# Ends of the expert blocks as a lane of jobs of their own, token-place sums on GpSimd, first projection one tick later: a two-layer transformer on one Trainium2 core

## The chip, the cores and the metric

The kernel runs on one core of a Trainium2 chip. The metric is device time in microseconds (us) of one execution; less is better. PE is TensorE, DVE is VectorE, ACT is ScalarE, POOL is GpSimd, SP is SyncE, which issues most DMAs. Each engine works through its own queue in order and waits for others by semaphores.

## The reference

Input is x, 2 sequences of 1024 tokens with 128 features, float32. Four sublayers follow one another, each with a residual and a layer norm behind it:

```python
x = _layernorm(x + _L0_attn_ref(x, ...))   # retention, 8 heads, decay, group norm, gate
x = _layernorm(x + _L0_ffn_ref(x, ...))    # causal attention of 16 heads of 8, then experts
x = _layernorm(x + _L1_attn_ref(x, ...))   # full attention of 16 heads of 8
x = _layernorm(x + _L1_ffn_ref(x, ...))    # product with a ternary 128x128 matrix
```

The second holds the part that is changed. After its attention it does, with a one-hot choice of one expert of four for every token:

```python
x = x + mla_attention(rmsnorm(x, norm1_w), Wq, Wdkv, Wuk, Wuv, Wo, ln_g, ln_b)
x = x + moe(rmsnorm(x, norm2_w), gate_w, gate_b, W1, b1, W2, b2)
...
h = jax.nn.relu(jnp.einsum('btd,ehd->bteh', x, W1) + b1)
y = jnp.einsum('bteh,edh->bted', h, W2) + b2
return jnp.einsum('bted,bte->btd', y, onehot)
```

## The kernel before, in words

Tokens go in tiles of 128, four tiles to a block of 512; block (b, k) is half k of sequence b. The retention runs first, chunk by chunk. From about 240 us on the kernel is a chain of **ticks** (chain_tick, line 553). A tick has one piece of scores for row maxima on PE (score, line 391; the maxima on DVE, lines 417 for pieces with the diagonal and 422 for whole ones), one piece of shifted, transposed scores that lies 7 pieces behind (shifted, line 455) with its exponentials on ACT (line 477), a mask on POOL for diagonal pieces of the causal attention (line 485), and the product of the piece before it with the values (line 502), whose result ACT copies out (tile part, two buffers, line 513) and POOL adds to oT (line 514). At the end of a group of heads come four transposes o_ps (line 524), a reciprocal and o_tok on DVE (lines 527, 528). Once a step's maxima are whole, ACT copies them to m_rows and SP brings them into qT by a DMA (line 444). All products go through eight PSUM banks in a ring: PE can't write a bank before DVE or ACT has read what was in it eight slots ago.

There are 208 pieces: ticks 0 to 79 start the causal attention's pieces, 80 to 207 the full attention's, where a block's full attention starts at 80 (b = 0) or 144 (b = 1). Ahead of every tick side_work (line 1393) steps the jobs of two lanes, heavy first, then light. A job is a generator; what it yields is the number of ticks until its next step. Only the first job of a lane steps, once in a tick unless it yields 0, and not before the jobs in its after list are done; a due time forces steps. Whatever a step issues stands in the engines' queues ahead of that tick's own work. Heavy holds experts(b, k) (line 1137) for the four blocks, light holds mla_inputs (the projections of sequence 1), attn_inputs (line 1290, which transposes the normalised block for the full attention at line 1302, projects it and spreads queries and keys by DMAs on SP, line 273) and outputs.

The stages of experts: project (transposes of o_tok, line 1059, then the product), residual xa on DVE; rmsnorm_T (line 238: square on POOL; sum ss on DVE, rstd and xn on POOL; transposes); gate product, choice of the expert oh and residual acc; places (line 1064), which counts with two products where each token goes in a list sorted by expert, in small DVE operations (lines 1078 to 1134); four scatters from POOL (line 1191), weights loaded by SP (line 1183); the sorted rows back, seven tiles of two products each (lines 1216 to 1238), the rows out. Then the **end** (lines 1260 to 1272): four gathers from POOL, an add to acc and the moments on DVE, rstd on POOL, and a tick later the normalising on DVE (line 228), which writes the input of the full attention.

By the program's order, the ticks of the ends are:

| block | gathers | add and moments | normalising | transposes of attn_inputs |
|---|---|---|---|---|
| (0,0) | 48, 49 | 50 | 51 | 52 |
| (0,1) | 73, 74 | 75 | 76 | 77 |
| (1,0) | 103, 104 | 105 | 106 | 107 |
| (1,1) | 133, 134 | 135 | 136 | 137 |

Blocks follow one another in the heavy lane: (0,0) steps from tick 22 to 52, (0,1) from 52 to 77, (1,0) from 77 to 107, (1,1) from 107 to 137. The counts of places come in ticks 29, 58, 84 and 114, the sums from them in the three ticks after.

Of the kernel before, what the change touches and what calls it, by code (L numbers as in the profile page):

```python
# [14 lines left out]
P = 128  # L15
# [49 lines left out]
def block_kernel(  # L65
# [66 lines left out]
    def col(name, i=0, rows_=P):  # L132
        at, _ = COLS[name]
        return cols_sb[:rows_, at + i : at + i + 1]
# [5 lines left out]
        nc.gpsimd.tensor_tensor(r, r, nhalf[:, :n], ALU.pow)  # L140
        return r

    def moments(parts):

        n = len(parts)
        st = small.tile([P, n, 6], F32, tag=f"st{n}", name="st")
        mv = small.tile([P, n, 2], F32, tag=f"mv{n}", name="mv")
        for i, part in enumerate(parts):
            nc.vector.bn_stats(st[:, i, :], part)
            nc.vector.bn_aggr(mv[:, i, :], st[:, i, :])  # L150
        return mv
# [48 lines left out]
    def flat(t):  # L200
        return t.rearrange("p c d -> p (c d)")
# [19 lines left out]
    def stats(parts):  # L221

        mv = moments(parts)
        return mv, rstd(mv[:, :, 1], len(parts), 1e-5)
# [7 lines left out]
    def tiles(t):  # L232
        return [t[:, c, :] for c in range(t.shape[1])]

    def scratch(tag, name, shape=(P, NC, P)):
        return scratch_of[0].tile(list(shape), F32, tag=tag, name=name)
# [819 lines left out]
    def project(src, w, name, got, tag):  # L1056
# [4 lines left out]
        yield 1  # L1061
        got["py"] = by_tile(oT, w, f"{name}_ps")

    def places(oh, found):

        def tiny(shape, name, dtype=F32):  # L1070
            return small.tile([P, *shape], dtype, tag=name, name=name, bufs=2)

        ps = slot("places")
        flat_oh = oh.rearrange("p c e -> p (c e)")
        mm(ps[:, : NC * NE], ahead, flat_oh)
        mm(ps[:, NC * NE : 2 * NC * NE], ones, flat_oh)
        got = tiny([2, NC, NE], "counts")
        nc.vector.tensor_copy(
            got.rearrange("p a c e -> p (a c e)"), ps[:, : 2 * NC * NE]
        )  # L1080
        rank_, total = got[:, 0], got[:, 1]
        for c in range(1, NC):
            nc.vector.tensor_tensor(total[:, c], total[:, c], total[:, c - 1], ALU.add)
        yield 1
        nc.vector.tensor_tensor(rank_[:, 1:], rank_[:, 1:], total[:, : NC - 1], ALU.add)
        some = tiny([NE, NC], "some")
        nc.vector.tensor_tensor(
            some, total[:, NC - 1].unsqueeze(2).to_broadcast([P, NE, NC]),
            filled.unsqueeze(1).to_broadcast([P, NE, NC]), ALU.is_gt,
        )  # L1090
        used = tiny([NE], "used")
        nc.vector.tensor_reduce(used, some, AX.X, ALU.add)
        prior = tiny([NE, NE], "prior")
        nc.vector.tensor_tensor(
            prior, earlier, used.unsqueeze(1).to_broadcast([P, NE, NE]), ALU.mult
        )
        base = tiny([NE], "base")
        nc.vector.tensor_reduce(base, prior, AX.X, ALU.add)
        at = tiny([NC, NE], "at")
        nc.vector.scalar_tensor_tensor(  # L1100
            at, base.unsqueeze(1).to_broadcast([P, NC, NE]), float(P), rank_, ALU.mult, ALU.add
        )
        nc.vector.tensor_tensor(at, at, oh, ALU.mult)
        where = tiny([NC], "where")
        nc.vector.tensor_reduce(where, at, AX.X, ALU.add)
        row_of = tiny([NC], "row_of", mybir.dt.uint32)
        nc.vector.tensor_copy(row_of, where)
        found["row_of"] = row_of
        yield 1
        begun = tiny([NT, NE], "begun")  # L1110
        nc.vector.tensor_tensor(
            begun, count.unsqueeze(2).to_broadcast([P, NT, NE]),
            base.unsqueeze(1).to_broadcast([P, NT, NE]), ALU.is_gt,
        )
        nth = tiny([NT], "nth")
        nc.vector.tensor_reduce(nth, begun, AX.X, ALU.add)
        expert_of = tiny([NT], "expert_of", mybir.dt.int32)
        nc.vector.tensor_scalar(expert_of, nth, -1.0, None, ALU.add)
        found["expert_of"] = expert_of
        yield 1  # L1120
        which = tiny([NT, NE], "which")
        nc.vector.tensor_tensor(
            which, nth.unsqueeze(2).to_broadcast([P, NT, NE]),
            count[:, :NE].unsqueeze(1).to_broadcast([P, NT, NE]), ALU.is_equal,
        )
        at_b1, _ = COLS["b1"]
        b1 = cols_sb[:, at_b1 : at_b1 + NE * NF].rearrange("p (e f) -> p f e", e=NE)
        picked = tiny([NT, NF, NE], "picked")
        nc.vector.tensor_tensor(
            picked, which.unsqueeze(2).to_broadcast([P, NT, NF, NE]),  # L1130
            b1.unsqueeze(1).to_broadcast([P, NT, NF, NE]), ALU.mult,
        )
        bias_1 = tiny([NT, NF], "bias_1")
        nc.vector.tensor_reduce(bias_1, picked, AX.X, ALU.add)
        found["bias_1"] = bias_1

    def experts(b, k, quick=False):

# [5 lines left out]
        xa = scratch("e_xa", "xa")  # L1146
        nc.vector.tensor_tensor(flat(xa), got["py"], flat(x1[b][k]), ALU.add)
        yield 0 if quick else 1
        yield from rmsnorm_T(xa, col("norm2"), got, "e_")
        xn, xnT = got["xn"], got["xnT"]  # L1150
        pg = by_tile(xnT, mw["gate"], "pgate")
        lg = small.tile([P, NC, NE], F32, tag="lg", name="lg")
# [8 lines left out]
        oh = small.tile([P, NC, NE], F32, tag="oh", name="oh")  # L1161
        nc.vector.tensor_reduce(top, lg, AX.X, ALU.max)
        nc.vector.tensor_tensor(oh, lg, top.unsqueeze(2).to_broadcast([P, NC, NE]), ALU.is_equal)
        nc.vector.tensor_tensor(oh, oh, rank.unsqueeze(1).to_broadcast([P, NC, NE]), ALU.mult)
        top2 = small.tile([P, NC], F32, tag="top2", name="top2")
        nc.vector.tensor_reduce(top2, oh, AX.X, ALU.max)
        nc.vector.tensor_tensor(oh, oh, top2.unsqueeze(2).to_broadcast([P, NC, NE]), ALU.is_equal)
        acc = scratch("e_acc", "moe_acc")
        nc.gpsimd.tensor_tensor(acc, x1[b][k], xa, ALU.add)
        yield 1  # L1170
        found = {}
        finding = places(oh, found)
# [6 lines left out]
        def load(i):  # L1179
            e = nc.sync.value_load(found["expert_of"][0:1, i : i + 1], min_val=0, max_val=NE - 1)  # L1180
            weights[i] = jobs_sb.tile([P, 2, FF], F32, tag="e_w", name="e_w", bufs=LEAD + 1)
            for a, name in enumerate(("w1", "w2")):
                nc.sync.dma_start(
                    out=weights[i][:, a, :], in_=m_w[:, bass.ds(e * FF + M_W[name][0], FF)]
                )

        yield next(finding)

        for c in range(NC):
# [59 lines left out]
        for i in range(NT + 1):  # L1249
# [7 lines left out]
                bias_2(i - 1)  # L1257
            yield 0 if quick and i % 2 == 0 else 1
        nc.sync.dma_start(out=from_expert.rearrange("(i p) d -> p i d", p=P), in_=rows_out)
        yield 2  # L1260
        made = scratch("e_xn", "e_made")
        for c in range(NC):
            nc.gpsimd.indirect_dma_start(
                out=made[:, c, :], out_offset=None, in_=from_expert, in_offset=indirect(c)
            )
            if c % 2:
                yield 1
        nc.vector.tensor_tensor(flat(acc), flat(acc), flat(made), ALU.add)
        mv, r = stats(tiles(acc))
        yield 1  # L1270
        apply(tiles(x2[b][k]), tiles(acc), mv, r)
        yield 1

    def ternary():
        wt = lw["wt"]
# [94 lines left out]
        Job(0, starts(0, 1, 0), mla_inputs(1, 0)),  # L1370
        Job(0, starts(0, 1, 1), mla_inputs(1, 1)),
    ]
    heavy = [Job(12, ends(0, 0, 0), clear())]
    for b in range(B):
        made = [Job(ends(0, b, k), starts(1, b, 0) - 3, experts(b, k, b == 0 and k > 0)) for k in range(NB)]
        heavy += made
        for k in range(NB):
            light.append(
                Job(ends(0, b, NB - 1), starts(1, b, 0), attn_inputs(b, k), made[k : k + 1])
            )  # L1380
    last_tick = n_items + AHEAD + 4
    for b in range(B):
        for k in range(NB):
# [4 lines left out]
                ]  # L1388
            else:
                light.append(Job(ends(1, b, k), last_tick, outputs(b, k)))  # L1390
    lanes = [heavy, light]

    def side_work(tick):
        for lane in lanes:
# [149 lines left out]
```

## Time and profile before

| what | us |
|---|---|
| median of three runs | 1108.45 (1107.76 to 1109.38) |
| the profiled execution | 1115.69 |
| its span, first to last instruction | 1113.9 |
| PE, DVE, ACT, POOL busy | 1034.0, 812.0, 677.8, 400.8 |
| DVE waiting for the DMA of a gather, line 1268 | 6.9 in 3 times |
| small sums on DVE for one block, lines 1085 to 1134 and 1164 | 3.5 |
| tick 75 in the table by tick, and tick 74 | 7.39 and 2.94 |

The profile is of one execution. Busy time of PE holds modelled ends of matmuls, so its share is high throughout; what tells is where it is idle, and the granted clock, which is 0.97 over the span and falls to one half for short intervals. A releaser in a row ("<-") is the last event before a wait ended.

### The profile page before, as it was taken

The numbers are of one execution on the slowest core, as the hardware profiler recorded it, in microseconds if no ns is written. First come the engines' busy times: TensorE is split into PE (matmuls) and PEld (weight loads), VectorE is DVE, ScalarE is ACT, GpSimd is POOL, SyncE is SP. The second block draws the span as 40 slices with busy tenths as digits, with TensorE's granted clock in tenths as the row PEclk, the third lists the DMA queues.
The fourth block names the chain that finished last, engine by engine and source line by source line (L and its number), as shares of the span: only waits on it lengthen the run. The fifth ranks groups of instructions, "written<-read, shape, count | busy, mean of one in ns | idle before, by whom it ended". The sixth has DMA issues, their size and how long they took to land.

```text
span 1113.9 us, 28817 instructions
## 1 busy us (share of the span) xinstructions
PE 1034.0 (93%) x11510; PEld 737.0 (66%) x11510; DVE 812.0 (73%) x1901; ACT 677.8 (61%) x1464; POOL 400.8 (36%) x498
## 2 busy tenths in 40 slices
PE   7999999988999899999989998999988989998995
PEld 5888888765666567666856675667755656665663
DVE  4667776767866867778678867787768888878871
ACT  3555544345666666556656766567656757776774
POOL 3466545523435533433443342233222121112122
PEclk9999999997999999889999999999989999999997
DMA  6511212100000231012301221112101000000000
GB/s 199 165 45 44 48 30 48 39 11 11 19 11 12 78 83 38 15 20 85 94 11 21 85 77 31 20 61 82 38 14 28 2 11 3 2 2 11 3 6 6
DMA packets 32214, 44.82 MB, mean 40 GB/s; under 512 B 4624, under 2 KB 18384, under 8 KB 31952
## 3 DMA queue, kind: packets, MB, share of 16 engines
q1 hardware_dynamic: 30816, 40.59, 13.7%
q0 software_dynamic: 1024, 2.10, 0.7%
q8 instruction: 91, 1.49, 0.6%
q14 instruction: 43, 0.35, 0.1%
q10 hardware_dynamic: 240, 0.29, 0.1%
HBM read 25.60 MB, written 4.39 MB: 27 GB/s over the span
## 4 chain that ended last, share of the span: by engine, by line
PE 66%; DVE 21%; POOL 5%; issue 3%; DMA 2%; ACT 2%; SPq 0%; DVEq 0%; POOLq 0%; ACTq 0%
PE acc L86 15%; PE sc L86 13%; PE sct L86 13%; DVE parts L422 6%; DVE spare L417 3%; PE ph L86 3%; PE pmoe L86 2%; PE pv L86 2%; PE pr L86 2%; PE py L86 2%; PE o_ps L210 2%; PE pout L820 1%; PE psc L86 1%; PE acc L436 1%; PE pg L86 1%
## 5 line engine op out<-in xcount | busy, mean ns | idle before, releaser
L477 ACT ACTIVATE es<-sct 128x512 f32<-128x512 f32 (+1 forms) x832 | 419.5, 586 | 185.8 <-PE sct L86 171.2
L422 DVE TENSOR_REDUCE parts<-sc 128x1 f32<-128x512 f32 x640 | 397.3, 683 | 112.0 <-PE sct L86 99.1
L86 PE MATMUL sc<-kT,qT 32*128 32x512 f32 (+3 forms) x1792 | 433.6, 586 | 2.4 <-ACT on L858 2.2
L86 PE MATMUL sct<-qT,kT 32*128 32x256 f32 (+1 forms) x3328 | 420.3, 391 | 2.2 <-DVE parts L422 1.4
L86 PEld LDWEIGHTS sct<-qT,kT 32*128 32x128 f32 x3328 | 301.8, 189 | 27.1 <-DVE parts L417 5.7
L86 PE MATMUL acc<-es,v_aug 128*32 128x256 f32 (+1 forms) x3328 | 221.1, 383 | 34.3 <-DVE parts L422 23.7
L514 POOL TENSOR_TENSOR oT<-oT,part 128x256 f32<-128x256 f32 x144 | 104.5, 726 | 405.4 <-ACT part L513 405.3
L86 PEld LDWEIGHTS sc<-kT,qT 32*128 32x128 f32 x1792 | 163.6, 190 | 69.3 <-DVE parts L422 23.1
L86 PEld LDWEIGHTS acc<-es,v_aug 128*32 128x32 f32 x3328 | 89.3, 110 | 134.9 <-DVE parts L422 62.4
L417 DVE CUSTOM_DVE_ANT_0 spare<-sc,causal 128x128 f32<-128x128 f32 (+3 forms) x256 | 125.6, 491 | 41.5 <-PE sct L86 10.9
L513 ACT COPY part<-acc 128x256 f32<-128x256 f32 x144 | 55.8, 388 | 28.1 <-PE acc L86 27.5
L888 ACT ACTIVATE og<-pt,cols_sb 128x128 f32<-128x128 f32 x124 | 45.1, 467 | 43.4 <-PE pt L875 43.4
L485 POOL TENSOR_SCALAR_AFFINE_SELECT es<-es 128x512 f32<-128x512 f32 x64 | 40.3, 636 | 72.4 <-ACT es L477 70.5
L140 POOL TENSOR_TENSOR rstd<-rstd,nhalf 128x4 f32<-128x4 f32 (+2 forms) x46 | 55.6, 1208 | 3.7
L774 ACT COPY v<-pv 128x1024 f32<-128x1024 f32 x16 | 16.2, 1012 | 38.1 <-PE pv L86 38.1
L751 POOL TENSOR_TENSOR swap<-swap,r_cs 128x1024 f32<-128x1024 f32 x15 | 35.4, 2357 | 10.4 <-DMA swap<-plain 10.3
L757 POOL TENSOR_TENSOR qd<-qk,r_rest 128x512 f32<-128x512 f32 x16 | 20.3, 1271 | 49.7 <-DVE qk L754 48.3
L86 PE MATMUL py<-r_wo,og 128*128 128x128 f32 x256 | 32.9, 284 | 2.0 <-DVE og L973 1.9
L86 PEld LDWEIGHTS py<-r_wo,og 128*128 128x128 f32 x256 | 31.2, 199 | 3.0 <-PE xn_ps L210 1.0
L820 PE MATMUL pout<-v,sm 128*128 128x128 f32 x256 | 31.5, 276 | 1.2 <-DVE sm L788 1.2
L86 PEld LDWEIGHTS ph<-xgT,e_w 128*128 128x128 f32 x224 | 27.0, 191 | 8.2 <-issue 3.9
L86 PE MATMUL pg<-xT,r_wg 128*128 128x128 f32 x256 | 31.4, 276 | 1.1 <-ACT v L774 1.1
(220 smaller groups left out, 1253.6 us busy)
## 6 DMA issues: line engine op xcount, KB each, us to landing
e_w<-in_m_w SPq DMA_DIRECT2D x56, 256.0 KB
swap<-plain SPq DMA_DIRECT2D x62, 128.0 KB
qT<-dense SPq DMA_DIRECT2D x32, 64.0 KB
kT<-dense SPq DMA_DIRECT2D x32, 64.0 KB
e_in<-by_expert SPq DMA_DIRECT2D x4, 448.0 KB
from_expert<-e_out SPq DMA_DIRECT2D x4, 448.0 KB
x<-in_x SPq DMA_DIRECT2D x4, 256.0 KB
mcs<-in_m_const SPq DMA_DIRECT2D x4, 256.0 KB
```

Source lines behind the costliest of these rows:

```text
L86: nc.tensor.matmul(o, lhsT, rhs, start=start, stop=stop)
L140: nc.gpsimd.tensor_tensor(r, r, nhalf[:, :n], ALU.pow)
L210: nc.tensor.transpose(tp[:, c * P : (c + 1) * P], src[:, c, :], ident)
L417: nc.vector.tensor_tensor_reduce(out=spare[:, :n], in0=sc[:, at : at + n], in1=causal[:, BT - n :], scale=1.0, scalar=-3.0e38, op0=ALU.add ...
L422: nc.vector.tensor_reduce(part, sc[:, at : at + n], AX.X, ALU.max)
L477: nc.scalar.activation(es[n_item][:, j, :n], sct[:, :n], AF.Exp, scale=scale)
L485: nc.gpsimd.affine_select(out=d, in_=d, pattern=[[0, GH], [1, P]], compare_op=ALU.is_ge, fill=0.0, base=0, channel_multiplier=-1,)
L513: nc.scalar.copy(part, acc[:, :BQ])
L514: nc.gpsimd.tensor_tensor(sum_, sum_, part, ALU.add)
L751: engine.tensor_tensor(swap[n], swap[n], table(n, 1), ALU.mult)
L820: nc.tensor.matmul(pout[n][:, a, g, :], sm[:, a, g, :], v[n][:, 2 * g + a, :], start=opens(n) and g == 0, stop=True, skip_group_check=True,)
L888: nc.scalar.activation(to, of, AF.Identity, bias=bias_, scale=weight)
```

## The change

It does five things. (1) The end of a block becomes a job endings in a lane closing, which stands between heavy and light; attn_inputs waits for it, and the next block's experts can run beside it. It has smaller stages: gathers in two ticks, the add, now on POOL, the moments in two ticks (in one where quick, block (0,1)), the normalising. No tick lies between that and the job's end any more, so attn_inputs starts in the tick of the normalising. (2) Most sums of places go to POOL; sums over four experts become two adds (added), and places takes one more stage. (3) experts starts one tick after the block's attention ends, for sequence 1 not before tick 80. (4) acc is made in a tick of its own, between xn and its transposes, and has a buffer for each k; the choice oh is split over two ticks with its product on POOL. (5) The gathers land in the buffer e_cols instead of e_xn.

```diff
+    def added(o, t):
+        at = (slice(None),) * (len(t.shape) - 1)
+        lower = t[(*at, slice(0, 2))]
+        nc.gpsimd.tensor_tensor(lower, lower, t[(*at, slice(2, 4))], ALU.add)
+        nc.gpsimd.tensor_tensor(o, t[(*at, 0)], t[(*at, 1)], ALU.add)
...
-        yield 1
-        nc.vector.tensor_tensor(rank_[:, 1:], rank_[:, 1:], total[:, : NC - 1], ALU.add)
         some = tiny([NE, NC], "some")
...
         nc.vector.tensor_reduce(used, some, AX.X, ALU.add)
+        yield 1
+        nc.gpsimd.tensor_tensor(rank_[:, 1:], rank_[:, 1:], total[:, : NC - 1], ALU.add)
         prior = tiny([NE, NE], "prior")
-        nc.vector.tensor_tensor(
+        nc.gpsimd.tensor_tensor(
             prior, earlier, used.unsqueeze(1).to_broadcast([P, NE, NE]), ALU.mult
         )
         base = tiny([NE], "base")
-        nc.vector.tensor_reduce(base, prior, AX.X, ALU.add)
+        added(base, prior)
+        row_base = tiny([NE], "row_base")
+        nc.gpsimd.tensor_scalar(row_base, base, float(P), None, ALU.mult)
+        yield 1
         at = tiny([NC, NE], "at")
-        nc.vector.scalar_tensor_tensor(
-            at, base.unsqueeze(1).to_broadcast([P, NC, NE]), float(P), rank_, ALU.mult, ALU.add
+        nc.gpsimd.tensor_tensor(
+            at, row_base.unsqueeze(1).to_broadcast([P, NC, NE]), rank_, ALU.add
         )
-        nc.vector.tensor_tensor(at, at, oh, ALU.mult)
+        nc.gpsimd.tensor_tensor(at, at, oh, ALU.mult)
         where = tiny([NC], "where")
-        nc.vector.tensor_reduce(where, at, AX.X, ALU.add)
+        added(where, at)
...
-        nc.vector.tensor_reduce(nth, begun, AX.X, ALU.add)
+        added(nth, begun)
...
-        nc.vector.tensor_scalar(expert_of, nth, -1.0, None, ALU.add)
+        nc.gpsimd.tensor_scalar(expert_of, nth, -1.0, None, ALU.add)
...
-        nc.vector.tensor_tensor(
+        nc.gpsimd.tensor_tensor(
             picked, which.unsqueeze(2).to_broadcast([P, NT, NF, NE]),
...
-        nc.vector.tensor_reduce(bias_1, picked, AX.X, ALU.add)
+        added(bias_1, picked)
...
-        yield from rmsnorm_T(xa, col("norm2"), got, "e_")
+        inputs_of = rmsnorm_T(xa, col("norm2"), got, "e_")
+        yield next(inputs_of)
+        yield next(inputs_of) - 1
+        acc = scratch(f"e_acc{k}", "moe_acc")
+        nc.gpsimd.tensor_tensor(acc, x1[b][k], xa, ALU.add)
+        yield 1
+        yield from inputs_of
...
-        nc.vector.tensor_tensor(oh, oh, rank.unsqueeze(1).to_broadcast([P, NC, NE]), ALU.mult)
+        nc.gpsimd.tensor_tensor(oh, oh, rank.unsqueeze(1).to_broadcast([P, NC, NE]), ALU.mult)
+        yield 0 if quick else 1
...
-        acc = scratch("e_acc", "moe_acc")
-        nc.gpsimd.tensor_tensor(acc, x1[b][k], xa, ALU.add)
...
+        ending.update(acc=acc, indirect=indirect)
+
+    def endings(b, k, ending, quick=False):
+
         yield 2
-        made = scratch("e_xn", "e_made")
+        acc, indirect = ending["acc"], ending["indirect"]
+        made = scratch("e_cols", "e_made", (P, NT, P))[:, :NC]
         for c in range(NC):
...
-        nc.vector.tensor_tensor(flat(acc), flat(acc), flat(made), ALU.add)
-        mv, r = stats(tiles(acc))
+        nc.gpsimd.tensor_tensor(flat(acc), flat(acc), flat(made), ALU.add)
+        yield 1
+        mv = small.tile([P, NC, 2], F32, tag="mv_e", name="mv")
+        for at in range(0, NC, 2):
+            moments(tiles(acc[:, at : at + 2]), mv[:, at : at + 2])
+            if at == 0 and not quick:
+                yield 1
+        r = rstd(mv[:, :, 1], NC, 1e-5)
         yield 1
         apply(tiles(x2[b][k]), tiles(acc), mv, r)
-        yield 1
...
-        made = [Job(ends(0, b, k), starts(1, b, 0) - 3, experts(b, k, b == 0 and k > 0)) for k in range(NB)]
-        heavy += made
+        after_ = (0, starts(1, 0, 0))
...
+        routed = [
+            Job(max(ends(0, b, k) + 1, after_[b]), by, experts(b, k, found_[k], quick[k])) for k in range(NB)
+        ]
+        made = [
+            Job(0, by + 1, endings(b, k, found_[k], quick[k]), routed[k : k + 1]) for k in range(NB)
+        ]
+        heavy += routed
+        closing += made
...
-    lanes = [heavy, light]
+    lanes = [heavy, closing, light]
```

The program's order after the change, in ticks: experts steps from 23 to 49, 51 to 71, 80 to 106 and 106 to 132; the ends are

| block | gathers | add | moments | normalising and transposes of attn_inputs |
|---|---|---|---|---|
| (0,0) | 51, 52 | 53 | 54, 55 | 56 |
| (0,1) | 73, 74 | 75 | 76 | 77 |
| (1,0) | 108, 109 | 110 | 111, 112 | 113 |
| (1,1) | 134, 135 | 136 | 137, 138 | 139 |

Each transpose of attn_inputs waits for its own tile's normalising. In the queue of POOL the next block's sq, rstd, xn and acc stand among the gathers and the add of (0,0) and (1,0). The counts of places come in ticks 31, 57, 88 and 114.

## The prediction, as it was put on record

> **What bounds the kernel now.** I read the page first, then a table by tick made from the instructions in order of time (a tick ends with the last weighted-values matmul, line 502), then the waits, the busy time by stretch and the timelines where TensorE pauses.
>
> ```profile
> PE 1034.0 (93%) x11510; PEld 737.0 (66%) x11510; DVE 812.0 (73%) x1901; ACT 677.8 (61%) x1464; POOL 400.8 (36%) x498
> ...
> PEclk9999999997999999889999999999989999999997
> ...
> PE 66%; DVE 21%; POOL 5%; issue 3%; DMA 2%; ACT 2%; SPq 0%; DVEq 0%; POOLq 0%; ACTq 0%
> ```
>
> TensorE is the bound: a quiet tick of the second attention takes 2.93 to 3.7 us, filled by PE, with 2.1 to 3.2 us of DVE in it. Time is lost only where PE pauses. Between ticks 22 and 147 (324 to 872 us, all that the change reaches) PE is idle 35.2 us. After a pause the granted clock falls to one half for 3.4 or 6.8 us, which costs half of that again. By stretch (columns: start and end, length, PE busy, PEld, DVE, ACT, POOL, granted clock, DMA share, GB/s):
>
> ```profile
> 324.25:339.15 14.90, 13.04 (x116) 8.76 (x116) 7.14 (x20) 7.64 (x16) 3.88 (x4) 0.89 0.05 6
> 366.00:376.90 10.90, 7.69 (x81) 4.83 (x82) 10.09 (x27) 4.90 (x11) 6.09 (x5) 0.84 0.25 61
> 453.80:470.70 16.90, 14.61 (x135) 9.41 (x136) 12.16 (x43) 8.25 (x19) 5.48 (x11) 0.80 0.05 10
> 488.50:504.70 16.20, 14.54 (x143) 9.90 (x140) 12.10 (x44) 7.07 (x16) 5.00 (x7) 0.79 0.01 2
> 566.60:579.00 12.40, 8.00 (x94) 5.31 (x95) 9.29 (x38) 4.50 (x11) 4.00 (x6) 0.86 0.04 12
> 690.75:702.50 11.75, 8.07 (x85) 4.86 (x85) 8.14 (x23) 4.82 (x12) 2.66 (x4) 0.85 0.08 17
> 813.75:826.80 13.05, 8.95 (x82) 5.16 (x82) 9.28 (x23) 5.12 (x11) 3.65 (x6) 0.74 0.04 12
> ```
>
> The loss of a stretch is its length less PE busy, plus (1 - clock) times the length: 3.5, 4.9, 5.7, 5.1, 6.1, 5.4 and 7.5 us, 38 in all. Smaller pauses of the same table by tick: 2.2 in ticks 25 and 26, 3.1 in tick 36 with its half-clock window, 3.1 in ticks 80 to 87, 2.0 in ticks 111 to 116, 0.5 in tick 61. Together **49 us** can be won at most. Why the four block ends (rows 3, 5, 6, 7) pause, shown at tick 75:
>
> ```profile
> 569.52 0.69 DVE L1268 TENSOR_TENSOR moe_acc<-moe_acc,e_made 128x512 f32<-128x512 f32 x1 [2.30 <-DMA e_made<-from_expert,row_of]
> 570.25 0.29 DVE L149 BATCH_NORM_STATS2 st<-moe_acc 128x6 f32<-128x128 f32 x1
> ...
> 571.76 0.18 DVE L150 BATCH_NORM_AGGREGATE mv<-st 128x2 f32<-128x6 f32 x1
> ...
> 572.64 0.64 PE L86 MATMUL acc<-es,v_aug 128*32 128x256 f32 x8 [4.40 <-DVE parts L417]
> ```
>
> DVE waits 2.30 us for the gather, adds 0.7, takes 1.9 for the moments, and only then the maxima that free PE's banks: PE stands 4.40 us.
>
> **The change part by part.** Ticks are those of the two programs.
>
> *The first projection a tick later.* At 326.69 PE had waited 1.86 us for o_tok (line 528) at the first transposes of tick 22; a tick later it is long there. 3.5 us shrink to 0.2. The step's whole chain, its eight transposes and products, moves with it; nothing else waits.
>
> *ss, rstd and xn apart from the same of mla_inputs.* In ticks 25 and 26 both run on POOL, the mask of line 485 stands behind them and PE waits 1.5 us for it. Now one pair per tick: 2.2 becomes 0.6.
>
> *Sums on GpSimd.* Per block these leave DVE, at the mean of their rows (lines 1085 to 1134 and 1164): 0.48, 0.47, 0.17, 0.24, 0.17, 0.17, 0.18, 0.28, 0.61, 0.27, 0.41, and the add of line 1268 0.69: 4.2 us, spread over more ticks. They add 16 small POOL operations of about 0.2 us (lines 139 and 1294 measure 0.19 and 0.20) with 0.1 between, and one add of 1.27 (row of line 1246): 6.1 us a block, 24 in all on an engine busy 36%. The form picked, 112 elements, has no POOL row: between 0.2 and 1.05 (line 1242, 512 elements), taken as 0.4, nearer in size to the small one. Left of the pauses of ticks 30, 31, 57 to 61, 80 to 87 and 111 to 116 (4.9 + 5.1 + 0.5 + 3.1 + 2.0 = 15.6): DVE keeps the counts, some and used in one tick (1.1 us) and waits in another for where on POOL before it can write row_of (0.2 to 1.4 us each, as POOL has a mask ahead or not): 1.4, 1.4, 1.0 and 0.9, so 4.7. Nearest rows for such a tick: 1.18 us idle in tick 140, where r3 and moments (2.6 us) come on top.
>
> One operation of these shows why moving helps twice:
>
> ```profile
> 490.17 1.13 DVE L1164 TENSOR_TENSOR oh<-oh,rank 128x16 f32<-128x16 f32 x1
> ```
>
> It took 1.13 us beside POOL's 1.27 (line 1169, 489.99), and the like ones before and after it 0.17. [...]
>
> *Tick 36.* There PE waits for the row maxima's DMA (line 444), which SP issues at 391.39 behind four spreads that waited for POOL's dense. The loads of weights move behind it, but POOL gets four sums and a scatter ahead of dense. 3.1 becomes 2.0 (0 to 4.5).
>
> *The ends.* The wait for the gather moves from DVE to POOL, where the tick's mask, oT's sum and the next rstd queue behind it, the moments a tick on and, but for block (0,1), over two ticks (0.95 us of DVE each), the normalising (four of 0.26, 1.1 us) into **the same tick as the transposes of attn_inputs**, which before came a tick after it. DVE ends a tick's maxima about 0.7 us after PE ends the tick (837.13 against 836.43), then 1.1, so the last transpose starts some 1.9 us into the tick instead of at 0.5: about 1.4 us of PE per block, on nothing's cover.
> - (1,1), alone in the lanes: gather lands 2.9 us into the tick of the add, add done at 4.2, a tick is 3.1: DVE waits 0.5 in the next. 0.4 + 1.4 + half of a clock window (0.8) = 2.6 instead of 7.5.
> - (0,1), also alone: eight diagonal maxima (3.6 us) in tick 75, then moments 1.9 in 76: PE waits 2.0 there, 1.5 at the transposes, 1.0 of clock: 4.5 instead of 6.1.
> - (1,0), beside the first stages of (1,1): POOL in tick 109 has rstd, xn and two gathers (1.3 + 1.1 + 2.5), then oT, in 110 acc and the add (1.3 each): the add ends about 9.4 us after tick 109 starts, but DVE meets the moments at 6.7. So DVE still waits about 2.7 us, PE 2.6 + 1.7 of clock; tick 113 has two more small DVE operations ahead of the normalising (2.2), plus 0.3. 6.8, with clock 7.5, instead of 5.4.
> - (0,0), beside (0,1): the same on POOL, with masks (1.25) in ticks 52, 53 and 55 behind sq, xn and the add; PE's products wait for the masks (about 2.5), tick 56 holds gate, a round trip of oh to POOL, the normalising and the transposes in a row (2.4), DVE's backlog 1.5, clock 2.6: 9.0 instead of 5.7.
>
> *Other.* acc gets two buffers, gathers land in the buffer of e_cols (read last four ticks before); attn_inputs' spreads come at tick 140 instead of 138 for queries of tick 144, and at 78 as before for tick 80, which paused 0.12: nothing. POOL late by a tick is covered by the two buffers of part.
>
> *Sum.* Left: 0.2 + 0.6 + 4.7 + 2.0 + 2.6 + 4.5 + 7.5 + 9.0 = 31.1, and 1.4 for small ones not seen: 32.5 of 49. **16.5 us won.** The profiled execution took 1115.69 (span 1113.9): 1099.2 for it, and 7.24 less, as the median lies, **1092 us**.
>
> **The rivals.**
> - *The lanes fit (0.17).* POOL catches up between ticks, since 36% of it is busy, and the two overlapped ends cost 3.5 each like the others: 9.5 us better, 1082. For it: tick 109's POOL work is an estimate from rows. Against: masks and xn in ticks 25 and 26 did hold PE.
> - *Only the small sums win (0.2).* In all four ends the wait passes from DVE through POOL back to DVE: ends 34 instead of 25, the rest wins 3.3 + 1.6 + 10.9 - 2 = 14, net 5: 1103. For it: moments need the add anyway, and the transposes' cover of one tick is gone.
> - *Slower: hand-overs to a late POOL (0.14).* Five times a block DVE now waits for a POOL result given in the same or the last tick (oh, where, nth, the add, rstd). If POOL stands more than about 0.7 us behind, which is the room that DVE has in a tick (2.94 - 2.28), the difference is a pause. With 1.3 us (one mask) each, 20 hand-overs cost 26, eight half-clock windows 14, against 24.7 of the ends and 10 of the rest that are gone: 5 us slower, about 1114. Decided by POOL's lag when its small sums are due. Against it: only the causal half of the ticks has masks.
> - *No lane of its own in half the blocks.* For (0,1) and (1,1) the heavy lane is empty while they end; this is in the sum, not a case of its own.
>
> **How the numbers follow.** Forecast 0.49, the lanes fit 0.17, only sums 0.2, slower 0.14. The range 1079 to 1110 reaches over the first three with their own spread (the term of tick 36, POOL's lag, 2.5 of normalising) and leaves out most of the last. About 0.2% (2.2 us) is what a measurement of this kernel tells from no change. Slower by more: 0.12, most of the last case. Within: 0.08. Faster: 0.80.
>
> **What would show it.** Right: no pause over 0.5 us in ticks 22 to 26; DVE never waiting for e_made's DMA; pauses of about 1.4 us at the transposes of line 1304's tick; PE idle of 324 to 872 us near 22 instead of 35; half-clock windows seven instead of eleven. Wrong: moments waiting on POOL by more than 3 us in all four ends, or PE's products waiting for masks in the scatters' ticks, would put it at the third or fourth case.

## The result, and the profile after

The changed kernel takes 1102.16 us (median of 14 runs, 1095.53 to 1110.10) against 1108.53 of before beside it (14 runs): ratio **0.9943**, interval 0.9924 to 0.9963, so 6.4 us less. In a later session before stood at 1113.98 and the changed kernel at 1103.83: 0.9896 (0.9878 to 0.9913), 10.2 us less. Forecast were 16.5 us. The level of before moved by 4 us between two sessions, even on the same chip, so kernels are compared below by their ratio to before in their own session.

The page of the profiled execution (1110.1 us, span 1108.4):

```profile
PE 1038.8 (94%) x11510; PEld 737.9 (67%) x11510; DVE 797.7 (72%) x1853; ACT 678.6 (61%) x1464; POOL 421.0 (38%) x566
...
PEclk9999999997997999989999999899999999999997
...
PE 70%; DVE 18%; POOL 5%; issue 3%; ACT 2%; DMA 2%; SPq 0%; POOLq 0%; DVEq 0%; ACTq 0%
...
L86 PE MATMUL sct<-qT,kT 32*128 32x256 f32 (+1 forms) x3328 | 419.0, 390 | 3.0 <-DMA qT<-m_rows 1.5
```

DVE is 14 us lighter, POOL 20 us heavier, as meant, and DVE's share of the chain falls from 21% to 18%. But the clock row has a dip in its thirteenth digit (333 to 360 us) that before does not have, and the last row says that shifted products waited for the DMA of the row maxima (its 1.5 us are those of tick 36; the wait in tick 22, below, stands under DVE). The busy time by stretch for the places that correspond to those shown of before, with the stretch between the third and the fourth (start and end, length, PE, PEld, DVE, ACT, POOL, granted clock, DMA share, GB/s):

```profile
326.70:344.00 17.30, 15.86 (x81) 9.23 (x85) 4.59 (x16) 6.18 (x12) 3.07 (x4) 0.61 0.03 4
366.50:376.90 10.40, 10.09 (x113) 6.54 (x112) 9.76 (x35) 6.50 (x14) 5.72 (x6) 1.00 0.04 14
456.40:473.00 16.60, 16.26 (x206) 11.51 (x206) 13.69 (x40) 9.93 (x25) 10.48 (x14) 1.00 0.07 19
473.00:482.80 9.80, 7.37 (x80) 4.63 (x75) 7.04 (x29) 4.87 (x10) 6.64 (x10) 0.83 0.01 2
482.80:497.10 14.30, 12.56 (x119) 8.68 (x115) 8.53 (x30) 6.12 (x14) 3.95 (x11) 0.88 0.07 16
568.50:581.20 12.70, 10.27 (x92) 6.38 (x90) 9.62 (x31) 5.54 (x12) 5.12 (x8) 0.87 0.01 2
705.00:723.40 18.40, 15.08 (x136) 9.54 (x134) 10.99 (x30) 8.30 (x17) 9.45 (x13) 0.72 0.03 8
811.90:830.70 18.80, 17.03 (x214) 10.83 (x210) 15.83 (x36) 12.54 (x28) 8.35 (x11) 1.00 0.06 16
```

The second and the last stretch run at full clock with 0.3 and 1.8 us of idle (length less PE busy): the sums of the places in ticks 30 and 31 are no longer felt, the end of block (1,1) little. The third runs at full clock too, but the end of (0,0) now falls behind it: in the fourth row PE pauses 2.43 us, all in tick 54, at 0.83 of the clock. The first got worse: 0.61 of the clock for 17 us.

Counted by ticks 22 to 147 of the two profiled executions (the granted clock changes in steps of 3.41 us, called windows here):

| | before | changed |
|---|---|---|
| length of the ticks | 547.3 | 539.0 |
| PE idle | 35.2 | 22.7 |
| lost to the half clock while PE is busy | 18.4 | 18.2 |
| half-clock windows | 11 | 11 |
| PE busy, in time at full clock | 493.7 | 498.0 |

The idle time fell as forecast (near 22). The half-clock windows did not, though seven were forecast, and the same 11510 matmuls take 4.3 us more of busy time. How two waits stood at one place in tick 22, first in before (SP's issues, then PE):

```profile
320.59 2.87 SPq L273 DMA_DIRECT2D qT<-dense  x4
323.56 0.56 SPq L444 DMA_DIRECT2D qT<-m_rows  x1
...
326.69 0.63 PE L210 MATMUL moT_ps<-ident,o_tok 128*128 128x128 f32 x4 [1.86 <-DVE o_tok L528]
...
327.77 1.22 PE L86 MATMUL sct<-qT,kT 32*128 32x256 f32 x4
```

and in the changed kernel (with DVE's maxima):

```profile
323.01 2.87 SPq L274 DMA_DIRECT2D qT<-dense  x4
325.98 0.56 SPq L445 DMA_DIRECT2D qT<-m_rows  x1
...
327.64 1.13 PE L86 MATMUL sc<-kT,qT 32*128 32x512 f32 x4
328.90 1.28 DVE L423 TENSOR_REDUCE parts<-sc 128x1 f32<-128x512 f32 x2
330.21 1.49 PE L86 MATMUL sct<-qT,kT 32*128 32x256 f32 x8 [1.44 <-DVE parts L423]
```

ACT copies m_rows at 318.2 in before and at 320.7 in the changed kernel; SP, in order, first issues four spreads that wait for dense, so the DMA goes out 5 us later. By its semaphore it lands 4.0 and 4.1 us after its issue (the median of the 64 such DMAs is 1.6). In before that is at 327.58, behind PE's 1.86 us for o_tok, and the shifted products start at 327.77 with no pause of their own. In the changed kernel nothing holds PE ahead of them, and they start after the DMA has landed (330.07). The row names DVE's maxima, which end at 330.18; PE waits here for the DMA's semaphore as well, and which of the two holds it is for the experiments to say. Four windows at half clock follow.

### The profile page after: what moved, and what is told of

Same layout as the page of the kernel before. It is cut to its first block, busy times and chain, and to the rows that moved or that the text cites. A ratio compares the mean times of both kernels' runs of the same rounds, so it can differ in the third digit from the quotient of the medians.

```text
span 1108.4 us, 28835 instructions
## 1 busy us (share of the span) xinstructions
PE 1038.8 (94%) x11510; PEld 737.9 (67%) x11510; DVE 797.7 (72%) x1853; ACT 678.6 (61%) x1464; POOL 421.0 (38%) x566
## 4 chain that ended last, share of the span: by engine, by line
PE 70%; DVE 18%; POOL 5%; issue 3%; ACT 2%; DMA 2%; SPq 0%; POOLq 0%; DVEq 0%; ACTq 0%
PE acc L86 16%; PE sc L86 15%; PE sct L86 14%; DVE parts L423 5%; PE ph L86 3%; DVE spare L418 2%; PE pmoe L86 2%; PE pr L86 2%; PE py L86 1%; PE pv L86 1%; PE mpr L86 1%; PE pout L821 1%; PE acc L437 1%; PE o_ps L211 1%; PE psc L86 1%
## 5 line engine op out<-in xcount | busy, mean ns | idle before, releaser
L758 POOL TENSOR_TENSOR qd<-qk,r_rest 128x512 f32<-128x512 f32 x16 | 20.4, 1273 | 50.1 <-DVE qk L755 47.3
L86 PE MATMUL pv<-r_wv,xT 128*128 128x512 f32 x64 | 30.5, 599 | 2.1 <-DVE qk L748 2.0
```

The lines of the kernel that those rows point to most:

```text
L86: nc.tensor.matmul(o, lhsT, rhs, start=start, stop=stop)
L758: nc.gpsimd.tensor_tensor(qd[n], rq[n], gq, ALU.mult)
```

## Experiments

Theory: the later projection uncovered the wait for the row-maxima DMA in tick 22, and what is left of the forecast gain went into it and the clock behind it. Rivals: DVE's eight diagonal maxima hold tick 22; the sums or the ends won less than forecast. All ratios are to before in the same session.

### 1. All 64 DMAs of the row maxima issued by ACT

```diff
-        nc.sync.dma_start(out=qT[b][ONE::HW, g, at : at + BQ], in_=rows_of)
+        nc.scalar.dma_start(out=qT[b][ONE::HW, g, at : at + BQ], in_=rows_of)
```

> The changed kernel, but the DMA that puts the row maxima into qT (line 445) is issued by ACT and no longer by SP, where four spreads stood ahead of it in ticks 22 and 36. Theory (the later projection only uncovered this DMA; PE waits for its landing): the pauses of 1.44 us in tick 22 and 1.47 us in tick 36 shrink below 0.4 us each, their half-clock windows (four after tick 22, one after tick 36) go too, and the time falls by 8 to 11 us, to about 1092. Rival (DVE's eight diagonal maxima of tick 22 hold PE, the DMA only lands at the same time): the pauses stay above 1.2 us and the time stays within 2 us of 1102. Second rival (the pauses go, but the half-clock windows after tick 22 come from something else): 3 us.

1114.77 us, ratio 1.0038 (1.0018 to 1.0058): slower than before. Yet tick 22 has no pause and tick 36 0.44 us, no half-clock window follows either, and ticks 22 to 36 last 65.9 us instead of 75.6. The loss is elsewhere: ticks 148 to 215 last 232.8 us, in the changed kernel 226.7. The group of this line, with shortest, median and longest time in ns:

```profile
L445 ACTq DMA_DIRECT2D qT<-m_rows x64: 527/538/1111, 248.7 to 1082.6; - x64
```

Each issue holds ACT's queue for 0.54 us, ahead of the exponentials that PE waits for. So the wait is shown to be the DMA's, and the remedy was too broad. An issue is 0.54 us of the 1.6 us to landing (medians of the 64 on ACT), a third, and 64 times on a busy engine it cost more than the 10 us that ticks 22 to 36 won. What the move saves in tick 22 is not this time but the 5 us behind the spreads.

### 2. The kernel before with the first projection a tick later

```diff
-        made = [Job(ends(0, b, k), starts(1, b, 0) - 3, experts(...
+        made = [Job(ends(0, b, k) + 1, starts(1, b, 0) - 3, experts(...
```

> The kernel before, with the first projection of a block's experts one tick later and nothing else of the change. The prediction gave this part 3.3 us in block (0,0). Theory (the wait for o_tok hid the wait for the row maxima's DMA): PE pauses about 1.4 us in tick 22 for that DMA instead of 1.86 for o_tok, half-clock windows follow as they did in the changed kernel, and the time is that of before within 2 us or up to 4 us slower. Rival (the part does what the prediction says, and tick 22 of the changed kernel suffers from another part): 3 to 4 us faster than before, 1105, and no pause over 0.5 us in tick 22.

1109.66 us, ratio 0.9990 (0.9966 to 1.0015): nothing. Tick 22 pauses 1.38 us, for the DMA now, with five half-clock windows. A second pause of 4.14 us is new, in tick 38, and stands against the gain too (SP, then PE):

```profile
397.42 4.30 SPq L1183 DMA_DIRECT2D e_w<-in_m_w  x6
401.82 0.39 SPq L1201 DMA_DIRECT2D e_in<-by_expert  x1
...
408.45 1.73 PE L1208 MATMUL xg_ps<-ident,e_in 128*128 128x128 f32 x7 [4.14 <-DMA e_in<-by_expert]
```

The six loads of weights now stand behind the second half's spreads and directly ahead of e_in on SP. In before they went out at 374.58, fourteen us before those spreads.

### 3. The moments of an end a tick later

```diff
         nc.gpsimd.tensor_tensor(flat(acc), flat(acc), flat(made), ALU.add)
-        yield 1
+        yield 1 if quick else 2
```

> The changed kernel, with the moments of a block's end two ticks and no longer one behind the add on POOL in blocks (0,0), (1,0) and (1,1) (not in (0,1)). Theory (DVE's queue stands behind the add that POOL does late, and PE stands behind DVE's maxima): the pauses of 3.32 us in tick 111 and 2.43 us in tick 54 fall below 0.6 us, with the half-clock windows behind tick 111, and the time falls by 6 to 9 us, to about 1095. Rival (POOL is late by more than a tick, or the pause only moves to the wait for the normalising): below 2 us.

1099.94 us, ratio 0.9902 (0.9866 to 0.9938), which overlaps the changed kernel's 0.9943 (0.9924 to 0.9963). In the changed kernel tick 111 is POOL's order, then DVE's, then PE's:

```profile
706.41 1.06 POOL L1285 DMA_INDIRECT e_made<-from_expert,row_of  x1 [0.16 <-issue]
707.77 0.95 POOL L1285 DMA_INDIRECT e_made<-from_expert,row_of  x1 [0.30 <-issue]
708.75 0.73 POOL L515 TENSOR_TENSOR oT<-oT,part 128x256 f32<-128x256 f32 x1
709.43 1.27 POOL L1164 TENSOR_TENSOR moe_acc<-x,xa 128x512 f32<-128x512 f32 x1
711.11 1.26 POOL L1290 TENSOR_TENSOR moe_acc<-moe_acc,e_made 128x512 f32<-128x512 f32 x1 [0.41 <-ACT es L478]
...
712.40 0.29 DVE L150 BATCH_NORM_STATS2 st<-moe_acc 128x6 f32<-128x128 f32 x1 [3.82 <-POOL moe_acc L1290]
...
713.94 1.93 PE L86 MATMUL acc<-es,v_aug 128*32 128x256 f32 x16 [3.32 <-DVE parts L423]
```

With the later moments this tick has no pause (3.53 us long instead of 7.78). But the moments' second half, the normalising and the transposes meet a little later: tick 114 is 8.38 us long with 1.86 idle. In block (0,0) nothing is won (46.8 us without the edit and 47.0 with it for ticks 51 to 60), since POOL itself, with its masks, is the late one there; the waits of tick 54 with the edit:

```profile
PE acc L86 <- POOL es L486: 1.9, 1, 1.9
```

The chain of waits was right, and half the gain moved on to the normalising.

### 4. A tick between the normalising and the transposes

```diff
         apply(tiles(x2[b][k]), tiles(acc), mv, r)
+        yield 1
```

> The changed kernel, with one tick between the normalising at a block's end and the transposes of attn_inputs in three of four blocks (the end of block (0,1) and its inputs share a later tick as before, by their due time). Theory (PE waits for the normalising in the same tick, the price that the prediction set at 1.4 us a block): the pauses of 1.74 us in tick 56 and those of tick 139 fall below 0.4 us, and the time falls by 3 to 5 us, to about 1098. Rival (the wait hides behind the moments, so that it goes elsewhere): below 1.5 us.

1101.29 us, ratio 0.9926 (0.9898 to 0.9955), where the changed kernel had 0.9943: less than expected and inside the error. The pause at the transposes,

```profile
485.95 1.01 PE L211 MATMUL x_ps<-ident,x 128*128 128x128 f32 x4 [1.74 <-DVE x L229]
```

is gone, but tick 56 still stands 1.38 us and tick 111 3.68 us, and ticks 113 to 116 last 17.9 us instead of 18.1: the transposes only moved to where other work is bound. Edit 3 takes away the wait for the add and keeps that for the normalising, edit 4 the reverse.

### 5 to 8. Two DMAs on ACT, by the wrong choice

```diff
+        queue = nc.scalar if steps[i] in ((0, 0, 1, 1, 0), (0, 0, 1, 3, 0)) else nc.sync
+        queue.dma_start(out=qT[b][ONE::HW, g, at : at + BQ], in_=rows_of)
```

in before (5), in before with the later projection (6), in the changed kernel (7), and there with the edits of 3 and 4 (8).

> The kernel before, with two of its 64 row-maxima DMAs issued by ACT: those of the steps (0,0,1,1,0) and (0,0,1,3,0), which stand behind spreads on SP in ticks 22 and 36. The other 62 stay on SP, since each cost ACT 0.54 us in the run with all of them there. Theory (in tick 22 two waits stand at the same place, o_tok and this DMA, and either hides the other): tick 22 keeps its pause of 1.9 us for o_tok, tick 36 loses its 1.4 us, and the time falls by 1 to 4 us against before, to about 1106. Rival (the DMA does not matter before the change): within 1 us of before, tick 36 pauses as it did.

> The kernel before with both edits: the first projection a tick later, and the two row-maxima DMAs of ticks 22 and 36 on ACT. Theory: both waits of tick 22 are gone, so that now the 3 to 4 us come that the prediction had given to the later projection alone: no pause over 0.4 us in ticks 22 to 25, and 3 to 7 us less than with the projection alone (1109.66), so 1103 to 1106. Rival (the tick is held by DVE's diagonal maxima too): a pause over 1 us stays in tick 22 and the time is within 2 us of 1109.

> The changed kernel with the two row-maxima DMAs of ticks 22 and 36 on ACT and the other 62 on SP. Theory: 1.4 us of pause in each of the two ticks goes, and the half-clock windows that follow some of the time; ACT loses only 2 x 0.54 us. 4 to 7 us less than the changed kernel: about 1097. Rival (what ACT does in these two ticks holds PE as much as the DMA did): within 1.5 us of 1102.

> The changed kernel with three edits: the two DMAs on ACT, the moments a tick later (blocks (0,0), (1,0), (1,1)), and a tick between the normalising and the transposes of attn_inputs. Theory (each of the three pauses has a cause of its own, and none hides another any more): the pauses of tick 22, 36 and 111 and the one at the transposes are below 0.5 us each, and the time is 8 to 14 us below the changed kernel, about 1091. Rival (DVE's and POOL's work that was done in the pauses now stretches the ticks beside them, so that gains do not add): 1096 or more.

Ratios 1.0014 (0.9999 to 1.0029), 0.9985 (0.9966 to 1.0005), 0.9925 (0.9897 to 0.9953) and 0.9855 (0.9825 to 0.9884). In 6, 7 and 8 the pause of 1.4 us stays in tick 22, in 5 the 1.86 us for o_tok. These two DMAs were not the delayed ones; the runs serve as controls: it is not the move of some DMA to ACT that helps. Number 8, with the edits of 3 and 4 together, is below each of them alone; its interval just overlaps that of 3, but its profile has one half-clock window from tick 22 to 147, where 3 has seven and 4 has three.

### 9 to 11. The three delayed DMAs on ACT

```diff
-        queue = nc.scalar if steps[i] in ((0, 0, 1, 1, 0), (0, 0, 1, 3, 0)) else nc.sync
+        queue = nc.scalar if steps[i] in ((0, 0, 1, 0, 1), (0, 0, 1, 2, 0), (0, 0, 1, 2, 1)) else nc.sync
```

in before with the later projection (9), in the changed kernel (10), and there with the edits of 3 and 4 (11).

> The runs with two DMAs on ACT had moved the wrong two: the time from ACT's copy of m_rows to its DMA is 0.3 us for these in the kernel before, and 5.4, 6.2 and 4.9 us for three others, of the steps (0,0,1,0,1), (0,0,1,2,0) and (0,0,1,2,1), which wait on SP behind spreads. Here: the kernel before, the first projection a tick later, and these three DMAs on ACT. Theory (tick 22 has two waits at one place, o_tok's and the DMA's): both are gone, no pause over 0.5 us in tick 22, and 3 to 5 us less than before on the same chip (ratio 0.9955 to 0.9975), where the projection alone gave 0.999. Rival (DVE's diagonal maxima hold the tick, whatever else is ready): a pause over 1 us stays in tick 22, ratio 0.998 to 1.000.

> The changed kernel with the three delayed row-maxima DMAs on ACT, the other 61 on SP. Theory: the pauses of 1.44 us in tick 22 and 1.47 us in tick 36 fall below 0.5 us each, and with them about half of the time a half-clock window of 1.7 us each: 3 to 5 us less than the changed kernel, ratio to before 0.990 to 0.992 where the changed kernel has 0.994. Rival (ACT's part or DVE's maxima take the place of the wait): within 1.5 us of the changed kernel.

> The changed kernel with the three delayed DMAs on ACT, the moments a tick later, and a tick between the normalising and the transposes. The last two of these, with the wrong DMAs, gave 0.9855 of before. Theory (causes add): 3 to 5 us less than that, ratio 0.981 to 0.983. Rival (with the last two the rest is bound by DVE in each tick, so that the pause of tick 22 only moves): 0.985 to 0.987.

Ratios **0.9933** (0.9911 to 0.9954), **0.9868** (0.9849 to 0.9888) and **0.9815** (0.9797 to 0.9834). Number 10, the line's group, and in tick 22 PE's rows and DVE's next maxima:

```profile
L446 ACTq DMA_DIRECT2D qT<-m_rows x1: 1110/1110/1110, 318.3 to 318.3; - x1
...
325.69 1.13 PE L86 MATMUL sc<-kT,qT 32*128 32x512 f32 x4
326.40 1.27 PE L86 MATMUL sct<-qT,kT 32*128 32x256 f32 x10
326.95 1.28 DVE L423 TENSOR_REDUCE parts<-sc 128x1 f32<-128x512 f32 x2
```

No wait at the shifted products, and they start (326.40) before those maxima begin (326.95), to which the changed kernel's trace put the wait: the rival falls. In all five profiles in which the delayed DMAs go out from ACT (1, 9, 10, 11, 15), ticks 22 to 25 last 18.6 us at full clock. The same ticks with the DMA on SP last 20.4 (number 4), 22.0 (3, 7, 8), 26.9 (changed kernel) and 28.5 us (13, 14), with none, one, four and five half-clock windows after the same pause of 1.4 us: 24.3 in the mean, so the one wait costs 5.7 us, and by chance between 2 and 10. (With numbers 2, 6 and 12, whose other stages are not those of the changed kernel: 24.0 in the mean of ten, 5.3 us.)

Number 9 against number 2 is the pair for the claim of two waits at one place: the later projection alone gives 0.1%, with the DMAs out of the way 0.7%, more than the 0.25 to 0.45% expected; the two were measured in different sessions, and their intervals do not meet. Number 11 has no half-clock window from tick 22 to 147. The clock row of its page:

```profile
PEclk9999999996899999999999999999999999999998
```

### 12 and 13. The sums back on DVE

In 12 with the stages of before (the function places, and the product of oh, as in before), in 13 with each changed line on DVE at its own tick:

```diff
-        lower = t[(*at, slice(0, 2))]
-        nc.gpsimd.tensor_tensor(lower, lower, t[(*at, slice(2, 4))], ALU.add)
-        nc.gpsimd.tensor_tensor(o, t[(*at, 0)], t[(*at, 1)], ALU.add)
+        nc.vector.tensor_reduce(o, t, AX.X, ALU.add)
```

> The changed kernel with the sums of the places, of base, of the bias pick and the product of oh with rank back on DVE, in the stages that before had (the lane of endings and the later projection stay). The prediction gave these sums on POOL 10.9 us of TensorE's pauses (15.6 to 4.7). If that holds, the pauses of ticks 28 to 33, 57 to 61, 80 to 92 and 111 to 118 come back, 8 to 11 us of idle, and the time is 1108 to 1112 on the first chip, ratio to before 0.999 to 1.004. Rival (the sums cost DVE what they cost, but the pauses came from the other work in these ticks, so most of the gain is the lane's): within 3 us of the changed kernel, ratio 0.993 to 0.997.

> The changed kernel, tick for tick, with the sums of the places on DVE instead of POOL. In the run with the sums on DVE in the stages of before, 4.37 us of pause stood in tick 38, where PE waited for e_in, whose DMA SP issued behind six loads of weights: the stages, not the engine, may have cost it its 8.8 us. Theory (the engine itself is worth little, the extra stages keep e_in out of the way): no pause in tick 38, 2 to 4 us of idle more in ticks 28 to 33, 57 to 61, 84 to 92 and 111 to 118 than the changed kernel, and 1 to 4 us more time than the changed kernel on the same chip. Rival (DVE's 4 us a block are what costs): 8 us or more.

Ratios 1.0022 (1.0007 to 1.0036) and 0.9942 (0.9925 to 0.9958), the changed kernel 0.9896 in the session of 13. Undoing engine and stages costs 0.8 to 1.3%, by which measurement of the changed kernel one takes, 9 to 14 us; undoing the engine alone 0.5%, some 5 us, between theory and rival. The rest is alignment: without the extra stages the loads fall ahead of e_in again (4.37 us in tick 38), and the end of (0,0) meets attn_inputs in tick 54 (9.96 us long, 3.62 of them idle). In the profiles of 13 and 14 the idle time is the same (22.6 and 22.2 us), so the 5 us of the engine are shown by the times and not by these pauses.

### 14 to 16. The changed kernel again; the lanes in another order; the projection back

14 is the changed kernel. 15 is number 11 with `lanes = [closing, heavy, light]`. 16:

```diff
-            Job(max(ends(0, b, k) + 1, after_[b]), by, experts(...
+            Job(max(ends(0, b, k), after_[b]), by, experts(...
```

> The changed kernel once more, so that the others of this chip have it beside them, since before stood at 1108 to 1110 on one chip and at 1114 to 1115 on another. Expected: ratio to before 0.992 to 0.996 as in its first measurement. If it is 0.988 or less here, the delayed DMAs' gain in the run with these on ACT (0.9868) is mostly the chip's; theory says it is not.

> The kernel with the three edits and the delayed DMAs (0.9815), with the lane of the endings ahead of the lane of the experts in each tick, so that on POOL and DVE a block's end stands ahead of the next block's first stages. Theory (the hand-over to POOL in tick 54 is late because rstd, xn and acc of the next block stand ahead of the add): the pause of 1.48 us in tick 54 shrinks below 0.8, 1 to 2 us less. Rival (the masks are late as much as before, only behind the add now): no change, within 1 us.

> The changed kernel with the first projection of each block's experts back in the tick of before. The prediction gave the later tick 3.3 us. Theory (in tick 22 the DMA's wait stands where o_tok's stood): tick 22 pauses for o_tok about 1.9 us instead of 1.44 for the DMA, within 2 us of the changed kernel, unless the moved stages bring e_in behind the loads again, which would show as a pause of over 2 us in ticks 37 to 39. Rival (the later tick is worth what the prediction said): 3 to 4 us slower than the changed kernel.

The two chips named there were no cause: the records name one chip for 1109.98 and for 1113.98 of before. 14 gives 0.9896, so its gain over before is larger here than in the first session, and number 10 lies 0.3% below it, some 3 us, with intervals that overlap. 15 gives 0.9818 (0.9801 to 0.9835), as number 11: tick 54 falls from 1.48 to 0.83, nearly as expected, but 2.9 us in tick 75 and 2.3 in tick 123 come in its place, so the time does not fall. 16 gives 0.9929 (0.9907 to 0.9950): the later projection is worth 0.3%, 3 to 4 us, in the changed kernel (its interval touches that of 14). The rival's number is right, but not its place: tick 22 pauses 1.85 us for o_tok then and 1.4 for the DMA otherwise. The gain is in ticks 26 to 36 (idle 6.4 us with the projection back, 2.9 without), where experts and mla_inputs meet.

**The best version** is number 11: 0.9815 of before, some 20 us, and about 0.8% below the changed kernel.

## Why the prediction was right in sign and wrong in size

Left after the change in its first profile, in the prediction's terms (us of PE idle, and half of each half-clock window):

| step | forecast | measured |
|---|---|---|
| the first projection a tick later | 0.2 | **8.3** |
| ticks 25 and 26 | 0.6 | 0.3 |
| sums on GpSimd | 4.7 | 3.5 |
| tick 36 | 2.0 | 3.2 |
| end (1,1) | 2.6 | 1.8 |
| end (0,1) | 4.5 | 4.2 |
| end (1,0) | 7.5 | 7.9 |
| end (0,0) | 9.0 | 7.9 |
| small ones | 1.4 | 3.8 |
| sum | 32.5 | 40.9 |

**The step that failed** is "3.5 us shrink to 0.2", with its reason "nothing else waits". Something else did: the shifted products of the same tick, for a DMA that landed 0.2 us before their turn. The prediction met the same DMA in tick 36 ("which SP issues behind four spreads"), and did not look for it in tick 22, where o_tok's wait hid it. In the profiles the term is 8.1 us off, as much as the difference between 16.5 forecast and the 8.3 us by which the ticks became shorter. That it fits so well is in part luck: this profile is of the slowest of the 14 runs, and two other errors cancel, 4.6 us more lost in before than counted and 4.3 us of busy time that came back (both below). In the mean over seven profiles of such a tick the wait costs 5.7 us, of the 6 to 10 us by which the timed gain fell short of 16.5; no run separates the rest. With this wait and most of that in tick 36 away (number 10) the ratio is 0.9868, 12 to 17 us: about the forecast, though in its later session the changed kernel itself had 10.

**"Half-clock windows seven instead of eleven"** failed with it: eleven, four of them behind tick 22 and three behind tick 111. The number is no property of the kernel: twelve in the second profile of the changed kernel, three in number 4 with nearly the same idle time (24.1 us).

**Ends and sums were right in size, and but for (0,0) in mechanism.** The four ends lose 21.8 us where 23.6 was forecast: DVE no longer waits for a gather, it waits for POOL's add in (0,0) and (1,0), and PE waits 1.4 to 1.7 us at the transposes in (0,0), (0,1) and (1,1). In tick 54 of (0,0) two waits again stand at one place: PE's pause ends with DVE's maxima at 476.3, the masks that the forecast named are done at 475.8, and they hold PE in number 3. No run shows the 2.5 us of normalising that the forecast's range counts with: at the two ends beside another block, (0,0) and (1,0), each normalising of the changed kernel took 0.34 to 0.35 us; at (0,1) and (1,1) the first of four, beside POOL's sum into oT of 0.72 us, took 0.88 and 0.79. The rival "only the small sums win" described (0,0) and (1,0) but not (1,1); the slower one, late hand-overs of the sums, did not come: no pause of ticks 28 to 33 or 84 to 92 is over 0.7 us. What the prediction took for the engine is in part the stages (12 against 13).

**What its count leaves out.** Of 12.5 us of idle removed, 4.3 came back as busy time. Tick 138, beside the quiet tick 134:

```profile
821.52:825.24 3.72, 3.72 (x44) 2.31 (x44) 3.62 (x12) 2.24 (x5) 1.96 (x3) 1.00 0.01 4
809.00:811.90 2.90, 2.90 (x42) 1.81 (x41) 2.45 (x5) 2.29 (x6) 1.82 (x3) 1.00 0.00 0
```

PE shows no idle time in either, yet the first takes 0.8 us longer, with 3.62 us of DVE in 3.72: DVE is the bound there, and PE's modelled ends cover the wait. Moments moved out of a pause into such a tick lengthen it. That this is all of the 4.3 us was not tested, and the figure itself is uncertain: the second profile of the changed kernel (14) has 502.0 us of busy time instead of 498.0, and before with two DMAs on ACT (5) has 499.6 instead of 493.7. On the other side, the loss of before, which the prediction counted at 49 us, is 53.6 by the count here (35.2 and 18.4).

## What to carry to other kernels

Before you price a wait that goes, list every wait of the same engine within the next few us and when each was satisfied: one satisfied 0.2 us before its turn takes the freed place. On an in-order issuing queue, compare the time at which a small DMA's data is ready with the time of its issue (here 5 us); a DMA behind others that still wait is moved singly, since each issue costs the new engine its own time (0.54 us here). Issuing it on SP ahead of the spreads would cost ACT nothing; no run tried that. Two edits that each hand their gain to the next wait must be tried together.

## What the runs showed of the hardware

In each of the 18 profiles the 7 to 23 changes of the granted clock (between 1.00 and 0.50 in before and the changed kernel) lie at whole multiples of 3.413 us from one another, to 3 ns. Windows at full clock between 30 and 1070 us of these profiles, by PE's idle time in them, and how many were followed by one at half clock:

| idle in the window | windows | half clock follows |
|---|---|---|
| under 1.0 us | 4975 | 6 |
| 1.0 to 1.25 | 117 | 9 |
| 1.25 to 1.5 | 52 | 23 |
| 1.5 to 2.0 | 49 | 38 |
| over 2.0 | 58 | 58 |

Of the windows with 1.25 to 1.5 us of idle time, 23 of 52 were followed by one at half clock, by the trace's record of matmuls. A pause of 1.4 us is a throw of dice, even where one window holds all of it: in tick 22 no half clock follows in number 4 (1.43 us in one window), four windows in the changed kernel (1.44 us). By the table (6 of 4975 windows under 1.0 us, 61 of 101 between 1.25 and 2.0) it is an estimate that two pauses of 0.7 us in different windows would cost almost no clock, and that four of 4 us turned into eight of 1.5 may keep their windows. In the mean over timed runs, the clock (span times what the granted clock lacks of 1) took 29.0 us from before (27 runs), 27.6 from the changed kernel (14) and 17.5 from number 11 (5), whose pauses are almost all under 1.25 us. In the changed kernel PE is idle for 0.00 us from 330.60 to 344.25 us (3.41 us busy in each window), yet all four windows are at half clock; products of 64 rows run there in tick 23 (336.38 to 341.86 us). Why the clock stayed at half is open.
